# Two transposes of a gated attention layer by 32x32 blocks and DRAM, a permuted token order of the residual, and a build-time clock that orders the stages

## The chip, the cores and the metric

The kernel runs on one core of a Trainium2 chip. That core has a matrix engine (TensorE; PE in the profile, with its weight loads shown apart as PEld), a vector engine (VectorE, DVE), an activation engine (ScalarE, ACT), a general engine (GpSimd, POOL) and a queue that issues DMAs (SyncE, SP). Each engine works through its own instructions in the order in which the program lists them; semaphores tie the engines together. The metric is the device time of one execution in microseconds (us), as a median of several runs.

## The reference

A layer norm without weights feeds an attention layer and a feed-forward layer in parallel, and both results are added to the input. There are 8 sequences of 256 tokens, width 256, 16 heads of 128, and 64 slots (`M`) per head. Cut to what matters:

```python
xn = (x - mean) / sqrt(var + 1e-5)
# attention, per head
q, k = rope(xn @ Wq.T), rope(xn @ Wk.T);  v = xn @ Wv.T;  g = xn @ Wg.T
s   = clip(xn @ Ws1.T @ Ws2.T + bs2, -32, 32)         # [T, 64]
es, enz = exp(s), exp(-cumlogsumexp(s over tokens))
A   = tril(q @ k.T) * 128**-0.5
ok  = enz * (A @ es)                                   # logits over 64 slots
qv  = softmax(ok)
W2  = tril((qv * enz) @ es.T)
o   = W2 @ v
o   = o * rsqrt(mean(o*o) + 1e-5) * g_norm * silu(g)
attn = concat_heads(o) @ Wo.T
# feed-forward, weights stored as 4-bit codes with one scale per 32
ffn = (gelu(xn @ Wgate.T) * (xn @ Wup.T)) @ Wdown.T
out = x + attn + ffn
```

All of it is computed in float32.

## The kernel before, in words

The 2048 tokens are cut into 4 groups of 512 (`G`), and a group into 4 chunks of 128 (`TC`). The heads are taken in pairs, so there are 4 groups x 8 pairs = 32 attention steps `n`. The steps are pipelined by hand: while step `n` computes values, gates, scores, logits and softmax, step `n + 1` gets its states and its rotated q and k, step `n - 1` gets its weights, outputs and so on, and `close` projects the outputs of an even and an odd step together. The feed-forward layer (`ffn`, L344) is a generator of 160 items (a gate block, an up block or a pair of down chunks each) that are dealt out among the steps. The 4-bit weights are decoded once into SBUF, 24 parts in all, in between.

**What sets the order.** The kernel schedules by hand: each stage function emits its matmuls at once, and puts what follows on the other engines into a `chain`, a generator that stops at `yield`. After each stage `tick` (L98) advances every open chain by one piece, in the order in which they were opened. `need` (L93) ticks until given chains are finished; `new` (L104) does so for the users of a buffer that is taken again, and the eight PSUM banks are such buffers (`bank`, L123). Within a step the stages are sorted by a place between 0 and 1, from the tables `POS`, `START`, `FEED`, `NORM_AT`; `FIRST`, `LAST` and `DUE` say how many feed-forward items and decoded parts each step gets.

**The logits and the softmax.** `logits` (L542) leaves 64 slots of two heads on the 128 partitions and 512 tokens along the free axis, and `ok` is that times `enz` (L560). The softmax needs tokens on partitions: `softmax` (L565) turns `ok` with four TensorE transposes of 128x128 into a PSUM bank (L572), takes the maxima (L580), and runs eight exponentials with their sums (L584). `turn` (L594), in the next step, transposes the result back with four more (L601) and multiplies it by `enz` (L605). `weights` (L632) waits for it.

**The outputs.** `outputs` (L674) applies the weights, normalizes and gates into `og` (L704), which has tokens on partitions. `turn_blocks` (L364) transposes its 32x32 blocks in place on VectorE (L366), and `exchange` (L368) moves the blocks to their places by a trip through DRAM: four stores of 64 KB (L371), and one load of 256 KB into `ogT` (L376). In `og` and `ogT` the four chunks of a token's place lie innermost, so that one chunk of `ogT` is read at a stride of four elements, which `close` does when it loads it as the weights of its matmuls (L728).

**Other lines that are named below.** `rope` (L462) projects q and k; `vg` (L514) values and gates; `ffn_block` (L298, L318) and `ffn_down` (L338) the feed-forward; `scores` (L532, L535); `states` (L424); `norm` (L205) the transposes of the normalized input into `xT`; `add_to` (L277) adds a PSUM bank to the residual `res`, and `added` (L266) stores two chunks when their last sum is in (L270); `load_w` (L161) loads a step's weights into a single buffer.

Of the kernel before, what the change touches and what calls it, by code (L numbers as in the profile page):

```python
# [32 lines left out]
POS = {'scores': (0.059, 0.112),  # L33
 'turn': (0,),
 'logits': (0.178,),
 'softmax': (0.232,),
 'cross': (0.179,),
 'weights': (0.179, 0.193),
 'low': (0,),
 'states': (0.223,),  # L40
 'outputs': (0.364, 0.394),
 'close': (0.107, 0.365),
 'rope': (0.36, 0.45, 0.487, 0.63),
 'vg': (0.458, 0.566, 0.766, 0.838)}
START = {-1: {'states': (0.544,), 'rope': (0.14, 0.43, 0.53, 0.63)},
 0: {'vg': (0.0, 0.03, 0.06, 0.229),
     'scores': (0.2, 0.28),
     'states': (0.342,),
     'logits': (0.34,),
     'softmax': (0.5,),  # L50
     'rope': (0.198, 0.24, 0.32, 0.45)}}
FEED = {-1: (0.452, 1.0)}
NORMS = {0: 1, 2: 2, 5: 3}
NORM_AT = (0.29, 0.293, 0.427, 0.58, 0.75, 0.938)
FIRST = [0.35, 1.41]
LAST = [2.16, 2.05]
DUE = [4, 6, 7, 7, 8, 8, 9, 10, 11, 12, 12, 13, 14, 15, 15, 16, 17, 18, 19, 19, 19, 22, 23, 23, 24]
# [3 lines left out]
def layer_kernel(ctx: ExitStack, tc: tile.TileContext, a: dict, out: bass.AP):  # L61
# [27 lines left out]

    chains = []  # L90
    held = {}

    def need(*gens):  # L93

        while any(c in chains for c in gens):
            tick()

    def tick():  # L98

        for c in list(chains):  # L100
            if next(c, chains) is chains:
                chains.remove(c)

    def new(pool, shape, tag, bufs=1, dtype=F32):  # L104

        users = held.setdefault(tag, [])
        if len(users) >= bufs:
            need(*users[-bufs])
        t = pool.tile(shape, dtype, tag=tag, name=tag, bufs=bufs)
        users.append([])  # L110
        at_tag[id(t)] = t, users[-1]
        return t

    at_tag = {}

    def chain(gen, *tiles):

        chains.append(gen)
        for t in tiles:
            at_tag[id(t)][1].append(gen)  # L120
        return gen

    def bank():  # L123
        return new(ps_p, [P, 512], "ps", 8)
# [24 lines left out]

    def load_x(t, k):  # L150

        nc.sync.dma_start(
# [4 lines left out]
    def load_w(n, k):  # L157

        if n < N:
            w = aw.tile([P, 2, 2, 2 * DK], F32, tag=f"wts{k}", name=f"wts{k}")  # L160
            nc.sync.dma_start(out=w, in_=a["wqkvg"][steps[n][1]][:, k : k + 2])  # L161
            wts[n, k] = w

# [20 lines left out]
    def norm(g, h):  # L184
# [5 lines left out]
        for i in range(2):  # L190
            nc.vector.bn_stats(st[:, i, :], res[:, g * TC + h + i, :])
            nc.vector.bn_aggr(mv[:, i, :], st[:, i, :])
        nc.vector.tensor_scalar(rstd, mv[:, :, 1], EPS, None, ALU.add)
        nc.gpsimd.tensor_tensor(rstd, rstd, nhalf[:, 0:2], ALU.pow)
        yield
        for i in range(2):
            nc.vector.tensor_scalar(
                xn[:, i, :], res[:, g * TC + h + i, :], mv[:, i, 0:1],
                rstd[:, i : i + 1], ALU.subtract, ALU.mult,
            )  # L200
        yield
# [6 lines left out]
        t = g * G + h * P  # L208

        def work():  # L210
            nc.scalar.copy(xT[:, :, t : t + 2 * P], ps.rearrange("p (c t) -> p c t", c=2))  # L211
            yield

        normed.setdefault(g, []).append(chain(work(), ps, xn))
        yield
# [6 lines left out]
    def load_packed(m):  # L222

        if m < 12:
# [4 lines left out]
            packed[m] = pk, sc  # L229

    def decode_next():
# [16 lines left out]
        def work():  # L248
            for k, left in enumerate((28, 24)):
# [3 lines left out]
            yield  # L253
            nc.vector.tensor_scalar(u, u, 0x81C00000 - (1 << 32), None, ALU.bitwise_and)
            nc.vector.scalar_tensor_tensor(
                w, u.bitcast(F32), 2.0 ** 126, sc.unsqueeze(1).to_broadcast([P, 2, CH]),
                ALU.mult, ALU.mult,
            )

        parts.append(chain(work(), pks, scs, u))  # L260
# [5 lines left out]
    def added(t):  # L266

        done[t] = done.get(t, 0) + 1
        if done[t] == left:
            nc.sync.dma_start(  # L270
# [610 lines left out]
```

## Time and profile before

| what | us |
|---|---|
| median of 3 runs (1251.34 to 1254.29) | 1252.76 |
| the profiled execution | 1250.65 |
| its span in the trace | 1248.6 |
| DVE busy | 866.9 (69%) |
| ACT busy | 508.5 (41%) |
| POOL busy | 442.4 (35%) |
| TensorE clock granted | 0.999 of full speed |

The span is the time from the first to the last instruction of the trace; some 2 us of the profiled execution's own time lie around it. A float32 matmul shows as two instructions, so that counts of matmuls in the rows are twice those in the code (the transposes are not doubled). The duration of a matmul is the time from its start to a modelled end, and successive matmuls overlap; what a matmul costs the engine is therefore read from start to start.

### The profile page before, as it was taken

What the parts mean: (1) busy time and instruction counts of PE and PEld (TensorE: products, weight loads), DVE (VectorE), ACT (ScalarE), POOL (GpSimd) and SP (SyncE); (2) the same over time, 40 slices, a digit from 0 to 9 for tenths busy, and PEclk for the clock granted to TensorE, in tenths of its full rate; (3) what the DMA queues carried; (4) which work ended last, traced back from release to release, by engine and by line L of the source; (5) the groups of instructions that cost most, each with busy time, mean ns of one, the idle gap of its engine ahead of it and who ended that gap; (6) DMA issues with size and microseconds to landing.
All of it is one profiled execution on the core that took longest, in us unless ns stands there. A gap on an engine that the chain in (4) does not pass through costs nothing.

```text
span 1248.6 us, 18213 instructions
## 1 busy us (share of the span) xinstructions
PE 1222.9 (98%) x6448; PEld 889.8 (71%) x6448; DVE 866.9 (69%) x1656; ACT 508.5 (41%) x1645; POOL 442.4 (35%) x408
## 2 busy tenths in 40 slices
PE   6999899999999999999999999999999999999997
PEld 3566677777777777767777686776777777777775
DVE  4987667786676778675787757766766677676553
ACT  3354334444344444343443534345443244444321
POOL 3525344333244432334442333444232344332311
PEclk9999999999999999999999999999999999999999
DMA  5104222112222212122221122222112222211211
GB/s 159 64 11 142 85 69 85 26 50 78 85 69 68 84 27 59 53 68 85 78 60 35 54 64 85 68 68 53 33 51 69 68 68 68 63 41 51 67 51 51
DMA packets 64514, 81.55 MB, mean 65 GB/s; under 512 B 7140, under 2 KB 44388, under 8 KB 64424
## 3 DMA queue, kind: packets, MB, share of 16 engines
q1 hardware_dynamic: 63992, 80.13, 22.5%
q8 instruction: 51, 0.84, 0.3%
q14 instruction: 39, 0.32, 0.1%
q10 hardware_dynamic: 432, 0.26, 0.1%
HBM read 61.49 MB, written 18.87 MB: 64 GB/s over the span
## 4 chain that ended last, share of the span: by engine, by line
PE 92%; DVE 4%; DMA 2%; issue 1%; ACT 1%; POOL 0%; ACTq 0%; SPq 0%; DVEq 0%; POOLq 0%
PE ps L514 17%; PE ps L462 17%; PE ps L728 10%; PE ps L338 9%; PE ps L318 8%; PE ps L298 8%; PE ps L683 4%; PE ps L532 4%; PE ps L551 4%; PE ps L642 3%; PE ps L535 2%; PE ps L424 2%; PE ps L572 1%; PE ps L619 1%; DMA pk<-in_codes_dram 1%; PE ps L668 1%
## 5 line engine op out<-in xcount | busy, mean ns | idle before, releaser
L475 POOL TENSOR_TENSOR z<-z,sin 128x512 f32<-128x512 f32 x128 | 164.3, 1284 | 380.7 <-ACT z L472 380.2
L462 PE MATMUL ps<-xT,wts 128*128 128x512 f32 x512 | 242.7, 597 | 0.7 <-ACT xT L211 0.7
L514 PEld LDWEIGHTS ps<-wts,xT 128*128 128x128 f32 x1024 | 194.3, 190 | 65.1 <-issue 37.5
L514 PE MATMUL ps<-wts,xT 128*128 128x256 f32 x1024 | 236.5, 379 | 0.0
L462 PEld LDWEIGHTS ps<-xT,wts 128*128 128x128 f32 x512 | 94.0, 191 | 79.3 <-issue 71.3
L471 ACT COPY z<-ps 64x512 f32<-64x512 f32 x128 | 74.5, 582 | 138.4 <-PE ps L462 80.3
L728 PE MATMUL ps<-w_o,ogT 128*128 128x256 f32 x512 | 127.0, 402 | 0.0
L728 PEld LDWEIGHTS ps<-w_o,ogT 128*128 128x128 f32 x512 | 122.5, 328 | 2.3 <-issue 1.2
L298 PE MATMUL ps<-xT,w_gate 128*128 128x512 f32 x256 | 120.7, 594 | 2.7 <-DVE q L473 2.7
L318 PE MATMUL ps<-xT,w_up 128*128 128x512 f32 x256 | 120.6, 593 | 0.4 <-DVE k L473 0.4
L338 PE MATMUL ps<-w_down,inter 128*128 128x256 f32 x512 | 116.4, 380 | 4.4 <-DVE inter L326 4.4
L451 DVE RECIPROCAL enz<-enz 128x128 f32<-128x128 f32 x128 | 116.7, 932 | 0.0
L306 POOL TENSOR_SCALAR t<-t 128x512 f32<-128x512 f32 x64 | 40.4, 631 | 213.9 <-ACT t L304 206.4
L338 PEld LDWEIGHTS ps<-w_down,inter 128*128 128x128 f32 x512 | 96.1, 190 | 18.9 <-DVE inter L326 5.6
L277 DVE TENSOR_TENSOR res<-ps,res 128x512 f32<-128x512 f32 x64 | 43.2, 679 | 82.4 <-PE ps L338 46.8
L476 POOL TENSOR_TENSOR k<-k,z 128x512 f32<-128x512 f32 x64 | 81.5, 1273 | 48.2 <-DVE k L473 44.8
L700 POOL TENSOR_TENSOR ss<-ss,nhalf 128x4 f32<-128x4 f32 x64 | 64.8, 1014 | 94.0 <-DVE ss L699 92.0
L704 DVE SCALAR_TENSOR_TENSOR og<-ps,ss,sgate 128x128 f32<-128x128 f32 x256 | 78.4, 434 | 19.8 <-POOL ss L700 19.8
L310 ACT ACTIVATE t<-t 128x512 f32<-128x512 f32 x64 | 40.3, 630 | 123.7 <-DVE t L308 123.7
L476 POOL TENSOR_TENSOR q<-q,z 128x512 f32<-128x512 f32 x64 | 81.5, 1273 | 21.7 <-DVE q L473 15.8
L308 DVE TENSOR_TENSOR t<-ps,t 128x512 f32<-128x512 f32 x64 | 43.3, 677 | 55.3 <-POOL t L306 55.3
L584 ACT ACTIVATE pr<-ps,mx 128x64 f32<-128x64 f32 x256 | 76.2, 323 | 12.8 <-DVE mx L581 10.4
(79 smaller groups left out, 1931.8 us busy)
## 6 DMA issues: line engine op xcount, KB each, us to landing
wts<-in_wqkvg_dram SPq DMA_DIRECT2D x64, 512.0 KB, 4.5
by_way<-og SPq DMA_DIRECT2D x256, 64.0 KB, 1.8
ogT<-by_way SPq DMA_DIRECT2D x64, 256.0 KB, 2.7
pk<-in_codes_dram SPq DMA_DIRECT2D x12, 256.0 KB, 10.3
sc<-in_scales_dram SPq DMA_DIRECT2D x12, 256.0 KB, 10.3
w_o<-in_wo_dram SPq DMA_DIRECT2D x4, 512.0 KB, 5.5
out_dram<-res SPq DMA_DIRECT2D x8, 256.0 KB, 2.2
res<-in_x_dram SPq DMA_DIRECT2D x3, 512.0 KB, 10.2
```

The source lines that it names most:

```text
L298: nc.tensor.matmul(pg, lhsT=w_gate[:, c, ns], rhs=xT[:, c, gs], start=c == 0, stop=c == 1)
L318: nc.tensor.matmul(pu, lhsT=w_up[:, c, ns], rhs=xT[:, c, gs], start=c == 0, stop=c == 1)
L338: nc.tensor.matmul(ps[:, k, :], lhsT=inter[g, n][0][:, (i + k) * P : (i + k + 1) * P], rhs=w_dn[:, n, :], start=n == 2 * q, stop=n == 2 * ...
L451: nc.vector.reciprocal(r, r)
L462: nc.tensor.matmul(ps, lhsT=w[:, c, :], rhs=xT[:, c, g * G : (g + 1) * G], start=c == 0, stop=c == 1)
L471: nc.scalar.copy(z[0:64], pv[64:128])
L475: nc.gpsimd.tensor_tensor(z, z, sin_b, ALU.mult)
L476: nc.gpsimd.tensor_tensor(y, y, z, ALU.add)
L514: nc.tensor.matmul(ps[:, k, :], lhsT=xT[:, c, tt], rhs=w[:, which, c, :], start=c == 0, stop=c == 1,)
L584: nc.scalar.activation(pr[:, k, :], pv[:, k, :], AF.Exp, bias=mx[:, k : k + 1], scale=SCALE, accum_out=sm[:, k : k + 1],)
L704: nc.vector.scalar_tensor_tensor(og[:, :, i], po[:, i, :], ss[:, i : i + 1], sg[:, i, j * DK : (j + 1) * DK], ALU.mult, ALU.mult,)
L728: nc.tensor.matmul(ps[:, k, :], lhsT=ogT[hh][0][:, :, i + k], rhs=w_o[:, (hp // 2) * 4 + hh, :], start=hh == 0, stop=hh == 3,)
```

## The change

The change has four parts.

**1. The logits and the softmax are turned by blocks and DRAM.** The eight TensorE transposes of a step, the stage `turn` and the two PSUM banks go. A helper `turned` does what `turn_blocks` and `exchange` did (one 32x32 block transpose on VectorE, four stores, one load), and is used for `ok`, for the exponentials `pr` and for `og`. The maxima are taken in two instructions from SBUF and the exponentials read SBUF. The multiplication by `enz` after the way back moves from VectorE to GpSimd. The four tiles involved have one buffer each, and two of them are taken again within the chain (`again`).

**2. The blocks are contiguous.** `og`, `ogT`, `ok` and `pr` are laid out as (block, chunk, 32), so that the transpose reads and writes runs, and `close` reads each chunk of `ogT` contiguously. The tokens of a chunk come out in another order, so the residual `res` and `x` use that order (the host permutes `x`); `inter` is written permuted, `xT` is written back in the natural order in two copies of ScalarE instead of one, and the final store of two chunks is eight stores of 32 rows instead of one.

**3. A clock at build.** A chain now yields the engine and an assumed cost before each piece, each stage adds an assumed TensorE cost, and pieces are emitted in the order of their assumed start times, up to the assumed TensorE time; `need` moves that time forward. Ranks (0 to 2) break ties. The clock exists at build only; the chip sees another order of the same kinds of instructions. The tables of places, `FIRST`, `LAST`, `NORM_AT` and `DUE` have other values.

**4.** A factor of 0.5 moves from the product of the feed-forward into the decoded down weights.

```diff
-POS = {'scores': (0.059, 0.112),
- 'turn': (0,),
- 'logits': (0.178,),
- 'softmax': (0.232,),
- 'cross': (0.179,),
- 'weights': (0.179, 0.193),
+POS = {'scores': (0.057, 0.067),
+ 'logits': (0.14,),
+ 'softmax': (0.303,),
+ 'cross': (0.15,),
+ 'weights': (0.182, 0.257),
...
+    def V(n):
+        return "v", 0.15 + 0.00105 * n
+    def S(n):
+        return "s", 0.15 + 0.00088 * n
+    def pe(t):
+        clock["pe"] += t
+    def begin(c):
+        if isinstance(c.what, Chain):
+            return float("inf") if c.what in chains else max(c.at, c.what.at)
+        return max(clock[c.what[0]], c.at)
+    def advance(until=None):
+        while chains:
+            c = min(chains, key=lambda c: (begin(c), c.rank))
+            t = begin(c)
+            if until is not None and t > until:
+                return
+            if isinstance(c.what, Chain):
+                c.at = t
+            else:
+                e, cost, *lag = c.what
+                clock[e] = t + cost
+                c.at = t + cost + (lag[0] if lag else 0.1)
+            c.what = next(c.gen, None)
+            if c.what is None:
                 chains.remove(c)
+            if until is None:
+                return
+    def need(*cs):
+        while any(c in chains for c in cs):
+            advance()
+        clock["pe"] = max([clock["pe"]] + [c.at for c in cs])
...
-            nc.scalar.copy(xT[:, :, t : t + 2 * P], ps.rearrange("p (c t) -> p c t", c=2))
+            for c in range(2):
+                nc.scalar.copy(xv[:, c, :, h : h + 2], pv[:, c])
...
         if done[t] == left:
-            nc.sync.dma_start(
-                out=out[t * P : (t + 2) * P, :].rearrange("(i p) d -> p i d", p=P),
-                in_=res[:, t : t + 2, :],
-            )
+            yield "d", 0.9
+            for k in (t, t + 1):
+                rows = out[k // TC * G : (k // TC + 1) * G].rearrange("(i r k) d -> r i k d", i=4, r=4)
+                for i in range(4):
+                    nc.sync.dma_start(
+                        out=rows[k % TC, i], in_=res[32 * i : 32 * (i + 1), k, :]
+                    )
...
-            nc.vector.scalar_tensor_tensor(it, t, 0.5, pu, ALU.mult, ALU.mult)
+            nc.vector.tensor_tensor(
+                it.rearrange("p (r i k) -> p i r k", r=4, i=4),
+                t.rearrange("p (i r k) -> p i r k", r=4, i=4),
+                pu.rearrange("p (i r k) -> p i r k", r=4, i=4), ALU.mult,
+            )
...
-    def turn_blocks(t):
-        v = t.rearrange("p (c k) i -> p c i k", c=4)
-        nc.vector.transpose(v, v)
-    def exchange(to, t):
+    def turned(to, t):
+        yield "v", 0.8
+        flat = t.rearrange("p c i k -> p (c i k)")
+        nc.vector.transpose(flat, flat)
+        yield "d", 1.75, 2.6
         by_way = dram.tile([P, 4, 32 * TC], F32, tag="by_way", name="by_way", bufs=4)
         for r in range(4):
             nc.sync.dma_start(
                 out=by_way.rearrange("(c k) r x -> r k c x", c=4)[r],
-                in_=t[32 * r : 32 * (r + 1)].rearrange("p (c k) i -> p c (k i)", c=4),
+                in_=t[32 * r : 32 * (r + 1)].rearrange("p c i k -> p c (i k)"),
             )
-        yield
+        yield "d", 0.4, 4.2
         nc.sync.dma_start(
-            out=to.rearrange("p t i -> p (t i)"), in_=by_way.rearrange("p r x -> p (r x)")
+            out=to.rearrange("p r i k -> p (r i k)"), in_=by_way.rearrange("p r x -> p (r x)")
         )
...
+        pe(0.86)
         of[n][tag, j] = y, chain(work(), ps, y, z)
...
-        ok = to["ok"] = new(p1, [P, G], "ok")
-        def work():
-            nc.vector.tensor_tensor(ok, ps, enz, ALU.mult)
-            yield
-        to["logits"] = chain(work(), ps, ok, enz)
+        ok = new(p1, [P, 4, TC, 32], "ok")
+        okT = to["okT"] = new(p1, [P, 4, TC, 32], "okT")
+        def work():
+            yield V(512)
+            nc.vector.tensor_tensor(
+                ok.rearrange("p c i k -> p i c k"), ps.rearrange("p (i c k) -> p i c k", i=TC, c=4),
+                enz.rearrange("p (i c k) -> p i c k", i=TC, c=4), ALU.mult,
+            )
+            yield from turned(okT, ok)
+        pe(1.4)
+        to["logits"] = chain(work(), ps, ok, okT, enz, rank=0)
     def softmax(n):
-        need(to["logits"])
-        ps = bank()
-        for i in range(TC):
-            ts = slice(i * P, (i + 1) * P)
-            nc.tensor.transpose(ps[:, ts], to["ok"][:, ts], ident)
...
+            yield to["logits"]
+            for j in range(2):
+                yield V(256)
+                nc.vector.tensor_reduce(
+                    mx[:, j * TC : (j + 1) * TC],
+                    okT[:, 2 * j : 2 * j + 2].rearrange("p c i k -> p i c k"), AX.XY, ALU.max,
+                )
+            yield "v", 0.17
             nc.vector.tensor_scalar(mx, mx, -SCALE, None, ALU.mult)
+            pr = again(p1, [P, 4, TC, 32], "ok", to["softmax"])
+            for j in range(2):
+                yield "s", 2.16
+                for i in range(TC):
+                    k, js = j * TC + i, slice(2 * j, 2 * j + 2)
+                    nc.scalar.activation(
+                        pr[:, js, i, :], okT[:, js, i, :], AF.Exp, bias=mx[:, k : k + 1],
+                        scale=SCALE, accum_out=sm[:, k : k + 1],
+                    )
...
-    def turn(n):
-        need(to["softmax"])
-        for i in range(TC):
-            nc.tensor.transpose(ps[:, i * P : (i + 1) * P], prf[:, i * P : (i + 1) * P], ident)
-            nc.vector.tensor_tensor(prT, ps, enz, ALU.mult)
+            prX = again(p1, [P, 4, TC, 32], "okT", to["softmax"])
+            yield from turned(prX, pr)
+            yield "g", 1.27
+            prT = to["prT"] = again(p1, [P, G], "prT", to["softmax"])
+            nc.gpsimd.tensor_tensor(
+                prT.rearrange("p (i c k) -> p i c k", i=TC, c=4),
+                prX.rearrange("p c i k -> p i c k"),
+                enz.rearrange("p (i c k) -> p i c k", i=TC, c=4), ALU.mult,
+            )
...
     def weights(n):
-        need(to["turn"])
+        need(to["softmax"])
...
-                    ps[:, k, :], lhsT=ogT[hh][0][:, :, i + k],
+                    ps[:, k, :], lhsT=ogT[hh][0][:, i + k],
...
-            tick()
+            advance(clock["pe"])
```

## The prediction

> **What bounds the kernel.** I read the first two blocks of the page, then busy time by stretch, then TensorE's timeline.
>
> ```profile
> PE 1222.9 (98%) x6448; PEld 889.8 (71%) x6448; DVE 866.9 (69%) x1656; ACT 508.5 (41%) x1645; POOL 442.4 (35%) x408
> ...
> PE   6999899999999999999999999999999999999997
> ```
>
> TensorE looks full from the third slice to the last but one. The stretches (busy us of each engine) say how full:
>
> ```profile
> 0.00:35.00 35.00, 24.40 (x79) 13.43 (x80) 18.42 (x36) 9.52 (x15) 13.52 (x22) 1.00 0.48 147
> 35.00:70.00 35.00, 30.71 (x132) 17.99 (x130) 33.39 (x68) 15.26 (x39) 15.35 (x14) 1.00 0.16 54
> 70.00:140.00 70.00, 66.36 (x358) 46.39 (x359) 52.79 (x107) 31.37 (x103) 32.01 (x29) 0.98 0.34 106
> 140.00:600.00 460.00, 460.00 (x2503) 340.27 (x2501) 327.44 (x626) 191.68 (x630) 161.64 (x145) 1.00 0.22 61
> 600.00:1100.00 500.00, 500.00 (x2662) 368.24 (x2662) 348.52 (x663) 211.31 (x691) 185.43 (x165) 1.00 0.22 63
> ```
>
> From 140 us on TensorE has no idle time, and its list of waits between 140 and 1226 us is empty. So in 32 pipelined steps (22 of them, from the `close` at 363.32 to that at 1169.36 in the chain of waits, take 806.04 us, or 36.64 each) a microsecond of TensorE work is a microsecond of the span, and work elsewhere is free until it makes TensorE wait. Idle are 18.5 us before 140 us (35 - 24.40, 35 - 30.71, 70 - 66.36; 7.4 are the wait for the first input) and 3.3 us near the end (L338, below).
>
> Busy time overstates what a matmul costs, since successive ones overlap. The timeline of TensorE (start, length, group) gives the cost from start to start:
>
> ```profile
> 616.70 3.62 PE L514 MATMUL ps<-wts,xT 128*128 128x256 f32 x16
> 620.15 1.88 PE L298 MATMUL ps<-xT,w_gate 128*128 128x512 f32 x4
> 621.87 0.60 PE L601 MATMUL ps<-ident,pr 128*128 128x128 f32 x4
> 622.31 0.60 PE L532 MATMUL ps<-q,k 128*128 128x256 f32 x2
> ...
> 630.82 0.66 PE L572 MATMUL ps<-ident,ok 128*128 128x128 f32 x4
> 631.32 1.88 PE L462 MATMUL ps<-xT,wts 128*128 128x512 f32 x4
> ```
>
> **Removed: the eight transposes.** L601 takes 0.44 us (621.87 to 622.31), L572 0.50 (630.82 to 631.32). 0.94 x 32 steps = **30.1 us**, all on the path. The 1.9 us for which L601 waits (before 140 us) go with it; behind them stand L532's own inputs, so I count them gone, with 0 as the other bound.
>
> **Contiguous weights of `close`.** These rows differ only in the stride of the operand:
>
> ```profile
> L728 PEld LDWEIGHTS ps<-w_o,ogT 128*128 128x128 f32 x512 | 122.5, 328 | 2.3 <-issue 1.2 <-DVE inter L326 0.2
> L338 PEld LDWEIGHTS ps<-w_down,inter 128*128 128x128 f32 x512 | 96.1, 190 | 18.9 <-DVE inter L326 5.6 <-issue 1.0
> ```
>
> In the chain of waits 16 matmuls of L728 take 3.84 us and 16 of L338 3.46. With the load at 190 ns the first should cost what the second does: 0.38 x 32 groups = **12.2 us**. Here a rule speaks against the change: the Trainium skill ("TensorE: Matmul & The Clock Gate", "LDWEIGHTS (loading the stationary operand)") lets the time of a load depend on the number of columns alone, which is 128 in both rows; by it the stride costs nothing and the gain is 0. The trace has 328 against 190 ns; I take the row, and 0 goes into the range.
>
> A second rule is against the first part: "VectorE: DVE Perf Modes", "Rules for kernel authors", sends a 128x128 transpose to TensorE where PSUM may be the target, and keeps VectorE for blocks of 32x32. By it the 30.1 us stay and the detour only adds latency: the sum would be 1240. But TensorE is the engine with no idle time, and VectorE has 29% (327.44 of 460 us busy), so here the slower way is the cheaper one.
>
> **Added on VectorE.** Per step two block transposes. Nearest row: L366 at 1152 ns, read and written at a stride of four; contiguous ones should take between 0.69 (the 512-element L326 row) and 1.15. With the two of `og`, 128 at 0.69 to 1.15 minus 73.7 now: +15 to +74 us; two smaller maxima instead of one at most +22 (680 ns again); less 21.9 for L605. That makes 860 to 941 us of some 1210, at most 78%: not a bound. GpSimd gets 32 x 1.27 (the L476 row) = 41 us, to 40%. ScalarE's exponentials stay; eight extra halves of the `xT` copy are at most 5 us on 41%. The other reshaped products keep their element counts, and the factor 0.5 removes no instruction: nothing, covered by idle time on VectorE.
>
> **Added on the DMA queue.** Two trips per step: 256 stores and 64 loads more. A trip moves 0.5 MB, so 33.5 MB on top of 81.55; the queue's share of the engines rises from 22.5% to about 32%. SP issues per step 8 x 0.43 + 2 x 0.34 = 4.1 us more. These share SP with the weight loads (L161), which wait there for TensorE to let the buffer go (50.0 + 25.4 us in all, longest 13.2), and whatever is queued behind waits too.
>
> **The new wait, and its cover.** `weights` waited for the transposes; now it waits for a chain of nine pieces. From the trace: logits' matmuls 1.35 (626.74 to 628.09), product 0.69, trip 7.2 (the `og` transpose at 608.21 to its load issued at 612.68, plus 2.7 to landing), maxima 0.9 to 1.4, scaling 0.17, eight exponentials with their reads 8 x 0.54 = 4.3, `eps` 0.15, second trip 7.2, product on GpSimd 1.27: 23 to 24 us. Its cover is what TensorE does between `logits` at place 0.14 and `weights` at 0.182 of the next step: a whole step, 36.64 - (30.1 + 12.2) / 32 = 35.3 us, plus `cross` 0.54 and `states` 0.66 between them, 36.5. About 12 us are left for queueing on VectorE, ScalarE, GpSimd and SP. Without cover every microsecond costs 32. Single buffers of `ok` and `okT` ask for less: they are free again once the second trip has been read.
>
> **The order.** All else in the steady part can move only within the idle time of the other engines; TensorE cannot gain there (it waits for nothing) but can lose. One thing speaks against the new order: the clock prices `rope` at 0.86 where the timeline has 1.72 from start to start (L298, the same shape: 620.15 to 621.87), `close` at 1.73 against 3.84, `scores` at 0.65 against 1.3; shared-array stages such as `logits` (1.4 against 1.35) are right. The order is made for a TensorE about twice as fast, and so for a VectorE that lags behind it. Real slack is then larger than assumed, which favours no waits; but a piece that was put behind another one, because both were thought late, can keep a bank busy. I take 0; bounds: gain 11 (the 11.1 us idle before 140 us beyond the first input) plus 3.3 at the end, loss about 0.5 us per step, 16 (waits of TensorE on VectorE before 140 us are 0.3 to 2.3 us each).
>
> ```profile
> PE ps L205 <- DVE z L197: 10.3, 3, 7.4
> PE ps L338 <- DVE inter L326: 4.4, 3, 2.1
> PE ps L298 <- DVE q L473: 2.7, 2, 2.1
> ```
>
> These three are most of what TensorE waits for (us in all, times, longest); none lies between 140 and 1226 us.
>
> **The end.** The last sum ends at 1245.45, and one store (issue 0.43, 2.2 to landing) closes the span at 1248.6. Now eight follow each other: seven more issues at 0.43 (median of the L371 issues) = **+3.0**; bounds 2.1 (0.30 each) and 8.2 (1.17, the longest). The eight of the other half begin some 3.7 us earlier and are just out. Earlier groups' stores hide.
>
> **Sum**, against the profiled execution: 1250.65 - 30.1 - 12.2 - 1.9 + 3.0 = 1209.5. The median of the runs lies 2.1 higher, so I name **1210**.
>
> **Rivals.**
> A. As forecast, and the start gets better too, since loads of `x` and of the codes now have landing times in the clock and the first steps' places are new. For: 11.1 us idle there, 3.3 at the end. Against: the first codes land late whatever the order (10.3 us from issue), and every other piece competes with the start-up. Two thirds of the 14.4: 1200.
> B. TensorE waits in the steady part for pieces ordered by the wrong prices, 0.5 us a step: 1210 + 16 = 1226. For: the halved prices. Against: VectorE's 29% idle time.
> C. The stride doesn't matter (the rule above): 1210 + 12.2 = 1222.
> D, slower: the chain from `logits` to `weights` doesn't fit a step. Place: L642 waiting for the product on GpSimd. Price: 24 us plus queueing, 31 times over what passes 36.5. The gain of some 41 us is spent at 41 / 31 = 1.3 us, so from a chain of 37.8 us on it is slower. It takes, for instance, 6.2 us (the longest wait of a weight load for L514) ahead of each trip's stores and 3 us more at the hand-overs: 39.4, or 2.9 x 31 = 90, which makes 1300. For: single buffers, an in-order SP that now does four trips a step. Against: 12 us of slack.
> E. The blocks don't replace the transposes but leave the count of matmuls as it was: excluded by the code, which emits none in `softmax`.
>
> **Chances.** Forecast 0.55, A 0.17, B 0.13, C 0.07, D 0.08. The range **1197 to 1230** takes in A, B and C with the tail's bounds and leaves D out. A measurement of this kernel can tell 0.2% from no change (2.5 us, about the spread of the three runs). Only D is slower, 0.07 with 0.01 for a D that just balances: faster 0.92, same 0.01, slower 0.07.
>
> **What would show it.** TensorE instructions 256 fewer (6448 to 6192), as 128 + 128 transposes go. L728's successor: loads at 190 ns, 16 matmuls in 3.46 us. Busy 100% from about 140 us, no waits of the `weights` matmuls on GpSimd. Steps of 35.3 us. VectorE near 900 us, block transposes 0.7 to 1.15 us each. DMA bytes near 115 MB. Last store landing 5 to 6 us after the last sum. The prediction is wrong if `weights`, or banks behind VectorE, show waits in each step, or if the loads of `close` stay at 328 ns.

## The result, and the profile after

The changed kernel takes 1242.76 us (median of 4 runs, 1241.07 to 1243.06), the kernel before 1252.17 in the same comparison: ratio 0.992, 95% interval 0.9902 to 0.9937. It is faster, by 9.4 us where about 42 were forecast, and lies 12.8 us above the end of the range. The profiled execution took 1241.07 us, with a span of 1239.3.

The first two blocks of the page of the changed kernel, with its DMA queue and the two rows of `close` (L841, L728 before):

```profile
PE 1202.6 (97%) x6192; PEld 838.2 (68%) x6192; DVE 891.9 (72%) x1720; ACT 516.0 (42%) x1653; POOL 484.7 (39%) x440
...
PE   6899899999999999999999999899999999999996
...
PEclk9989999999999999999999999899999999999998
...
q1 hardware_dynamic: 110968, 113.71, 34.2%
...
L841 PE MATMUL ps<-w_o,ogT 128*128 128x256 f32 x512 | 115.7, 379 | 0.0
...
L841 PEld LDWEIGHTS ps<-w_o,ogT 128*128 128x128 f32 x512 | 96.5, 190 | 20.5 <-issue 8.1
```

The 256 instructions are gone (6448 to 6192), and the loads of `close` fell from 328 to 190 ns, so the work removed is the work forecast. But TensorE has a slice at 8 in the middle, and its granted clock dips in the same slice and near the start. Busy time by stretch of the changed kernel (columns as before: PE, PEld, DVE, ACT, POOL, then granted clock, DMA share, GB/s):

```profile
0.00:35.00 35.00, 25.25 (x80) 14.12 (x81) 18.32 (x37) 10.35 (x18) 13.86 (x23) 0.95 0.44 139
35.00:70.00 35.00, 28.94 (x112) 16.08 (x111) 34.59 (x67) 15.35 (x40) 15.11 (x14) 0.90 0.26 80
70.00:140.00 70.00, 64.24 (x345) 43.55 (x344) 56.05 (x115) 31.36 (x103) 36.49 (x33) 1.00 0.48 129
140.00:600.00 460.00, 459.33 (x2436) 324.59 (x2437) 346.42 (x661) 197.35 (x637) 182.70 (x160) 1.00 0.34 92
600.00:1100.00 500.00, 496.03 (x2607) 346.95 (x2606) 363.02 (x698) 217.72 (x698) 199.90 (x177) 0.99 0.35 92
```

From 140 to 1100 us TensorE now idles 4.6 us (0.67 + 3.97) where it idled 0, and the start got no better: from 35 to 70 us VectorE is busy 34.59 of 35 us, so there it is the bound, and TensorE does less in that time (28.94 us at a clock of 0.90, against 30.71 at 1.00). Its waits (us in all, times, longest):

```profile
PE ps L279 <- DVE z L261: 16.8, 3, 7.1
PE ps L423 <- DVE inter L407: 7.4, 5, 2.6
PE ps L515 <- DMA w_s<-in_ws_dram: 2.2, 1, 2.2
PE ps L423 <- DVE at L623: 1.9, 1, 1.9
```

None of them is the new chain. `weights` (L748) waits for nothing; GpSimd's product stands in front of its trip for 22.7 us in all, and TensorE does not feel it.

**Where the time went.** The start of each `close` in TensorE's timeline cuts the span into four: up to the first `close`, 28 steps, the last `close` but one to the last, the tail. These are profiled executions (that of the contiguous blocks alone was its slowest, 3.3 us above its median); the two kernels in the last rows come back in the experiments.

| | first close at | 28 steps (one) | to the last close | tail | span |
|---|---|---|---|---|---|
| before | 140.1 | 1029.1 (36.75) | 67.9 | 11.5 | 1248.6 |
| changed kernel | 155.1 | 1012.7 (36.17) | 57.7 | 13.8 | 1239.3 |
| contiguous blocks alone | 138.9 | 1020.1 (36.43) | 67.9 | 13.8 | 1240.7 |
| changed kernel, TensorE transposes back | 157.4 | 1038.0 (37.07) | 56.5 | 14.3 | 1266.2 |

Forecast was a step of 35.43 in these terms (36.75 less 0.94 and 0.38). Measured is 36.17: 0.74 x 28 = 20.7 us are missing there. The start took 15.0 us longer and the stretch to the last `close` 10.2 us less; together that is 4.8 longer where four steps' share of the gains should have made it about 5 shorter. Most of the two numbers is a shift of the cut itself: the new tables put the first `close` of a step at 0.348 of it instead of 0.107. Cut at `weights`, whose place hardly moved (0.179 to 0.182), the third of them starts at 149.0 us before and at 149.6 after, 28 steps take 1029.0 and 1014.5, and what follows takes 70.6 and 75.1 us. So the start brought nothing, and the end lost 4.5 us, the longer tail included.

### The profile page after: what moved, and what is told of

Its sections match the earlier page's. It is cut to its first block, busy times and chain, and to the rows that moved or that the text cites. A ratio compares the mean times of both kernels' runs of the same rounds, so it can differ in the third digit from the quotient of the medians.

```text
span 1239.3 us, 18558 instructions
## 1 busy us (share of the span) xinstructions
PE 1202.6 (97%) x6192; PEld 838.2 (68%) x6192; DVE 891.9 (72%) x1720; ACT 516.0 (42%) x1653; POOL 484.7 (39%) x440
## 4 chain that ended last, share of the span: by engine, by line
PE 86%; DVE 9%; DMA 2%; issue 1%; POOL 1%; ACT 0%; POOLq 0%; DVEq 0%; SPq 0%; ACTq 0%
PE ps L556 16%; PE ps L613 15%; PE ps L423 9%; PE ps L841 9%; PE ps L376 8%; PE ps L398 7%; PE ps L632 4%; PE ps L791 4%; PE ps L652 4%; PE ps L748 3%; PE ps L635 2%; PE ps L515 2%; PE ps L775 1%; DVE enz L543 1%; DMA pk<-in_codes_dram 1%
## 5 line engine op out<-in xcount | busy, mean ns | idle before, releaser
L556 PE MATMUL ps<-xT,wts 128*128 128x512 f32 x512 | 248.7, 609 | 0.5 <-ACT xT L289 0.5
L556 PEld LDWEIGHTS ps<-xT,wts 128*128 128x128 f32 x512 | 92.1, 192 | 79.6 <-issue 69.8
L423 PE MATMUL ps<-w_down,inter 128*128 128x256 f32 x512 | 122.0, 392 | 9.4 <-DVE inter L407 7.4
L695 ACT ACTIVATE ok<-okT,mx 128x64 f32<-128x64 f32 x256 | 85.6, 337 | 91.2 <-DVE mx L689 86.6
L398 PE MATMUL ps<-xT,w_up 128*128 128x512 f32 x256 | 123.1, 604 | 0.0
L572 POOL TENSOR_TENSOR q<-q,z 128x512 f32<-128x512 f32 x64 | 81.5, 1273 | 94.8 <-DVE q L569 69.7
L423 PEld LDWEIGHTS ps<-w_down,inter 128*128 128x128 f32 x512 | 98.9, 196 | 26.4 <-DVE inter L407 9.7
L841 PE MATMUL ps<-w_o,ogT 128*128 128x256 f32 x512 | 115.7, 379 | 0.0
L349 DVE TENSOR_TENSOR res<-ps,res 128x512 f32<-128x512 f32 x64 | 44.0, 688 | 93.9 <-PE ps L423 57.7
L841 PEld LDWEIGHTS ps<-w_o,ogT 128*128 128x128 f32 x512 | 96.5, 190 | 20.5 <-issue 8.1
L543 DVE RECIPROCAL enz<-enz 128x128 f32<-128x128 f32 x128 | 108.5, 909 | 0.0
L817 DVE SCALAR_TENSOR_TENSOR og<-ps,ss,sgate 128x128 f32<-128x128 f32 x256 | 75.3, 344 | 45.9 <-POOL ss L813 45.9
L566 ACT COPY z<-ps 64x512 f32<-64x512 f32 x128 | 74.5, 582 | 73.0 <-PE ps L556 63.8
L572 POOL TENSOR_TENSOR k<-k,z 128x512 f32<-128x512 f32 x64 | 82.6, 1290 | 20.6 <-DVE k L569 16.9
L623 DVE TENSOR_TENSOR at<-ps,mask 128x384 f32<-128x384 f32 x128 | 65.4, 552 | 26.4 <-PE ps L635 26.0
```

Source lines behind the costliest of these rows:

```text
L398: nc.tensor.matmul(pu, lhsT=w_up[:, c, ns], rhs=xT[:, c, gs], start=c == 0, stop=c == 1)
L423: nc.tensor.matmul(ps[:, k, :], lhsT=inter[g, n][0][:, (i + k) * P : (i + k + 1) * P], rhs=w_dn[:, n, :], start=n == 2 * q, stop=n == 2 * ...
L543: nc.vector.reciprocal(r, r)
L556: nc.tensor.matmul(ps, lhsT=w[:, c, :], rhs=xT[:, c, g * G : (g + 1) * G], start=c == 0, stop=c == 1)
L566: nc.scalar.copy(z[0:64], pv[64:128])
L572: nc.gpsimd.tensor_tensor(y, y, z, ALU.add)
```

## The experiments

The question is which part ate the gain: the trips, the clock at build, its prices, or the tables of places. A kernel is either in **the order of before** (one piece per chain after each stage), or **under the clock**, with the old or the new tables. Ratios are against the kernel before, with 95% intervals.

### Contiguous blocks alone

The kernel before with parts 2 and 4 of the change:

```diff
-        ogT = new(p2, [P, P, TC], "ogT", 4)
+        ogT = new(p2, [P, 4, TC, 32], "ogT", 4)
...
-                    ps[:, k, :], lhsT=ogT[hh][0][:, :, i + k],
+                    ps[:, k, :], lhsT=ogT[hh][0][:, i + k],
```

> The kernel before with the contiguous blocks alone (layout of og and ogT, token order of the residual, eight stores at the end); TensorE transposes and the old order stay. If the stride is a TensorE cost as the loads' rows say: 12.2 us less and 3 us more at the end, 1243 against 1252, and 16 matmuls of close in 3.46 us. If the stride costs nothing: 1252 to 1256.

1239.47 us, ratio 0.9898 (0.9881 to 0.9914). These two parts gain 12.7 us alone (against the 1252.17 of the result), more than the whole change does. In its timeline of TensorE 16 matmuls of `close` (L738 here) take 3.45 us from start to start, as forecast from L338:

```profile
650.49 3.62 PE L738 MATMUL ps<-w_o,ogT 128*128 128x256 f32 x16
653.94 0.59 PE L540 MATMUL ps<-q,k 128*128 128x256 f32 x2
```

So the rule weighed in the prediction (the Trainium skill, "TensorE: Matmul & The Clock Gate", "LDWEIGHTS (loading the stationary operand)"), that the columns alone set a load's time, does not hold for this stride, and rival C falls. Parts 1 and 3 on top of it made the kernel 3 us slower, though part 1 removes 30 us of TensorE's work.

### The changed kernel without the clock, and with true prices

First the tables of the change with the order of before's rule (one piece per chain after each stage), then the change with the clock told what TensorE really takes.

```diff
-            c = min(chains, key=lambda c: (begin(c), c.rank))
-            t = begin(c)
-            if until is not None and t > until:
-                return
+        for c in list(chains):
```

> The changed kernel with the old rule of order (after each stage every open chain advances by one piece) in place of the clock; all operations and the tables of places stay. Theory 1 (the order made by the clock loses what the transposes gave): 1210 to 1225, clearly under the changed kernel's 1242.8. Rival (the loss is in the operations themselves, as VectorE's longer work and the split TensorE sequence, whatever the order): 1235 to 1250. Rival 2 (the clock is what keeps TensorE fed): over 1250.

1312.22 us, ratio 1.0477 (1.0459 to 1.0494). With the new tables the clock is worth 69 us: these tables need it.

```diff
-        pe(0.86)
+        pe(1.72)
...
-        pe(1.73)
+        pe(3.46)
```

> The changed kernel with the clock's TensorE prices set to what the trace shows (1.72 for 0.86, 3.46 for 1.73, 1.3 for 0.65, 0.9 for 0.46). If pieces stand behind others because the clock takes TensorE for twice as fast: 1220 to 1232, and the waits near 58, 133 and 794 us shrink. If the order of pieces isn't what makes TensorE wait: 1240 to 1246.

1241.49 us, ratio 0.9907 (0.9892 to 0.9922), against 0.992 (0.9902 to 0.9937) for the change. The halved prices, on which I rested rival B, are not the cause. With true ones the waits near 794 us shrink to one of 0.9 us, but the two long waits of the start stay and shorter ones come elsewhere ("PE ps L652 <- DVE at L623: 4.7, 8, 1.3").

### The clock with TensorE's transposes

The change with its trips taken out again: eight TensorE transposes per step, the stage `turn`, two banks; then the same with the old tables.

```diff
-            yield from turned(okT, ok)
...
+            nc.tensor.transpose(ps[:, ts], to["ok"][:, ts], ident)
...
+            nc.tensor.transpose(ps[:, i * P : (i + 1) * P], prf[:, i * P : (i + 1) * P], ident)
```

> The changed kernel with the eight TensorE transposes of a step back, everything else (clock, tables, contiguous blocks) as changed. Theory 1 (the clock and its tables lose 28 us whatever they order): 1265 to 1272, slower than before. Theory 2 (the clock's order is as good as the old one, the loss comes with the trips): 1238 to 1244, as the contiguous blocks alone.

1268.19 us, ratio 1.013 (1.0113 to 1.0147).

> The sixth experiment's kernel (clock, contiguous blocks, TensorE transposes) with the tables of before, so that TensorE's own order is the old one and the clock orders the other engines alone; the norms keep two pieces, at 0.29 and 0.58 and their turns at 0.75 and 0.938. If the new tables (TensorE's order) cost the 28.7 us between the first and the sixth experiment: 1238 to 1246. If the clock's order of the other engines costs them: 1260 to 1275.

1255.94 us, ratio 1.0031 (1.0018 to 1.0044), between the two forecasts. Both do the same work as the contiguous blocks alone (1239.47), in another order. So with transposes the order costs 28.7 us: 16.5 by the clock with the old tables, 12.3 more by the new ones. And under the new order the trips are worth 1268.2 - 1242.8 = 25.4 us; a step falls from 37.07 to 36.17, by 0.90, against 0.94 forecast. The gain is there in the step; the order had taken it beforehand.

### The trips in the order of before

If the order costs that much, the trips should go into the old one. Chains of before stop only at `yield`; so each wait for a trip was put some idle ticks (n) behind the load.

The core of it, on top of the contiguous blocks alone, with the transposes and `turn` taken out:

```diff
+            turn_blocks(pr)
+            yield
+            yield from exchange(prX, pr)
+            for _ in range(n):
+                yield
+            nc.gpsimd.tensor_tensor(
...
```

Three idle ticks before the maxima and before the product, then none:

> The first experiment's kernel (contiguous blocks, old order and tables) with the eight TensorE transposes of a step replaced by the two trips through DRAM, three idle ticks before each use of what a trip brings. Theory 1 (the trips are worth 28 us, the loss is in the new order and tables): 1210 to 1222. Theory 2 (the trips themselves cost about what they save, since the longer chain and VectorE's extra pieces make TensorE wait and cool): 1232 to 1250.

> The fifth experiment's kernel without the idle ticks, so that VectorE's and GpSimd's uses stand where the trip has often not landed. If VectorE held up by a trip is what stalls TensorE: 10 us or more over the fifth. If there is slack for it: within 4 us of it.

1283.65 us, ratio 1.0259 (1.0239 to 1.0279), with three, slower than either forecast; 1396.57 us, ratio 1.117 (1.1132 to 1.1208), with none. The trips now cost 44 and 157 us. Waits of the kernel with three, of TensorE and of GpSimd:

```profile
PE ps L546 <- POOL k L490: 30.1, 13, 4.3
...
POOL prT L623 <- DMA okT<-by_way: 130.5, 29, 9.8
```

GpSimd's timeline in one step of it (start, length, group, idle time before it):

```profile
327.48 1.27 POOL L623 TENSOR_TENSOR prT<-okT,enz 128x512 f32<-128x512 f32 x1 [7.13 <-DMA okT<-by_way]
328.71 1.26 POOL L489 TENSOR_TENSOR z<-z,sin 128x512 f32<-128x512 f32 x1
330.05 1.27 POOL L490 TENSOR_TENSOR k<-k,z 128x512 f32<-128x512 f32 x1
331.27 1.26 POOL L489 TENSOR_TENSOR z<-z,sin 128x512 f32<-128x512 f32 x1
332.61 1.27 POOL L490 TENSOR_TENSOR q<-q,z 128x512 f32<-128x512 f32 x1
333.84 1.27 POOL L489 TENSOR_TENSOR z<-z,sin 128x512 f32<-128x512 f32 x1
335.19 1.26 POOL L490 TENSOR_TENSOR k<-k,z 128x512 f32<-128x512 f32 x1
```

The product stands 7.13 us in its wait; the six pieces of the rotation behind it start late, and TensorE's scores wait for the last of them. Without idle ticks VectorE stands in the same way ("DVE mx L599 <- DMA okT<-by_way: 113.6, 31, 5.5"). At this point two readings were left: the place of that wait, or something else that trips do to the old order.

### The same, with the product later

Only the number of idle ticks before the product changes, from three to eight and to fourteen; then eight with the product on VectorE.

```diff
-            for _ in range(3):
+            for _ in range(8):
                 yield
             nc.gpsimd.tensor_tensor(
```

> The order of before with contiguous blocks and both trips, as in the run at 1283.65 us, but the product on GpSimd is put eight ticks behind its trip instead of three. If what that order loses is GpSimd standing in the wait for the trip ahead of the pieces of the rotation (130.5 us of waiting there, TensorE's scores then 30.1 us late and its clock falling after each wait), the later place takes most of the 130.5 us away and the time falls towards that of contiguous blocks alone less the transposes: 1215 to 1245. If the trips cost the old order through something else (VectorE's larger load, the DMA queue), it stays within 10 us of 1283.

> As the run before, fourteen ticks behind. By the first theory no worse than with eight unless the weights stage is reached first, when the remaining ticks are run off in a row and the wait comes back: 1215 to 1260. By the second, near 1283.

> Eight ticks behind, but the product on VectorE (32 x 0.7 us more there, 41 us less on GpSimd). If only the place in the queue counts, the same as with eight ticks on GpSimd within 8 us. If GpSimd itself is short of time for the rotation, faster than that by over 8 us; if the wait now stands on VectorE ahead of the PSUM readers, slower.

| ticks before the product | us | ratio (95%) |
|---|---|---|
| 3, GpSimd | 1283.65 | 1.0259 (1.0239 to 1.0279) |
| 8, GpSimd | 1231.97 | 0.9828 (0.9809 to 0.9847) |
| 14, GpSimd | 1232.68 | 0.9838 (0.9824 to 0.9853) |
| 8, VectorE | 1231.23 | 0.9829 (0.9815 to 0.9844) |

One instruction put later takes 51.7 us away. GpSimd in the same step, with eight ticks:

```profile
320.93 1.28 POOL L490 TENSOR_TENSOR k<-k,z 128x512 f32<-128x512 f32 x1 [0.68 <-DVE k L487]
322.16 1.27 POOL L489 TENSOR_TENSOR z<-z,sin 128x512 f32<-128x512 f32 x1
323.51 1.26 POOL L490 TENSOR_TENSOR q<-q,z 128x512 f32<-128x512 f32 x1
325.80 1.26 POOL L623 TENSOR_TENSOR prT<-okT,enz 128x512 f32<-128x512 f32 x1 [1.02 <-DMA okT<-by_way]
327.02 1.26 POOL L489 TENSOR_TENSOR z<-z,sin 128x512 f32<-128x512 f32 x1
```

Pieces of the rotation now go ahead of it, and it waits 1.02 us. Its waits for the trip fall from 130.5 to 21.2 us in all, and L490 no longer stands in TensorE's list of waits. GpSimd is not short of time, since the product on VectorE gives the same. So the old order carries the trips, and the new one is not needed for them: with trips in both, the changed order stands at 1242.8 and the old one at 1232.0.

### Where the new order loses: places and waits

The same stretch of a step, TensorE's timeline of the changed kernel:

```profile
623.29 1.16 PE L748 MATMUL ps<-prT,esT 64*128 64x128 f32 x16
624.38 1.98 PE L556 MATMUL ps<-xT,wts 128*128 128x512 f32 x4
626.29 0.71 PE L775 MATMUL ps<-cross,prT 64*128 64x128 f32 x8
626.94 1.98 PE L556 MATMUL ps<-xT,wts 128*128 128x512 f32 x4
628.76 1.05 PE L791 MATMUL ps<-v,wt 128*128 128x128 f32 x8
```

and of the contiguous blocks alone (L650 and L676 are the same two stages):

```profile
623.60 1.16 PE L650 MATMUL ps<-prT,esT 64*128 64x128 f32 x16
624.60 0.61 PE L676 MATMUL ps<-cross,prT 64*128 64x128 f32 x8
625.14 0.38 PE L432 MATMUL ps<-w_s,rT 17*128 17x128 f32 x2
```

In the old order the stages that use 64 or 17 rows of the array stand together. The new one puts a stage of 128 rows (here `rope`) between them, and at every passage between the two kinds the start-to-start time is longer: L748 1.09 against 1.00 us, the first L556 1.91 against 1.72 (its usual distance), L775 0.65 against 0.54, the second L556 1.82. That is 0.09 + 0.19 + 0.11 + 0.10 = 0.49 us a step less 0.05 for a passage that the old order has too (L580 behind L432), some 12 us over 28 steps. The same distances stand in nearly every step. No wait shows it, and TensorE counts as busy. To test it, `apply` (L775) was put back beside `weights`; in a second run `states` was put behind both.

```diff
- 'weights': (0.182, 0.257),
+ 'weights': (0.182, 0.182),
```

The second run:

```diff
- 'weights': (0.182, 0.257),
+ 'weights': (0.182, 0.183),
...
- 'states': (0.167,),
+ 'states': (0.19,),
```

> The changed kernel with the second part of the weights stage (apply) at the place of the first (0.182 for 0.257), so that the matmuls of 64 rows stand together again. If each passage between matmuls of 64 and of 128 rows costs TensorE 0.1 to 0.2 us, as the start-to-start times suggest (0.3 us a step): 1232 to 1236. If not: 1240 to 1246.

> The changed kernel with weights at 0.182, apply at 0.183 and states at 0.19, so that cross, weights, apply and states stand side by side as before. If the passages between matmuls of part of the array and of all of it cost the 0.3 us a step that the start-to-start times show: 1233 to 1238. If not: 1240 to 1246.

1242.1 us, ratio 0.9912 (0.9897 to 0.9927): no gain. The two passages go, but `apply` now waits in the middle of its matmuls (0.34 us in one step) for VectorE to copy `states` out ("DVE esT L526") and takes 0.90 us from start to start on average instead of 0.65; and from 140 to 1100 us TensorE idles 13.0 us instead of 4.6. With `states` behind both 1324.07 us, ratio 1.0569 (1.0551 to 1.0588): there VectorE stands 119.6 us in the wait for `okT` (L684), and TensorE's scores wait 39.3 us for L572. Moving stages also moves the other engines' queues, so the passages could not be changed alone, and their 12 us stay a reading of the timeline, which no run confirms. What speaks for it: waits hardly tell the two kernels with trips apart. Behind the first input TensorE waits 22.6 us in the changed one and 22.7 in the old order with the product eight ticks late, at 10.5 and 8.1 us of lost clock (worked out at the end), yet 28 steps take 1012.7 and 1004.0 us.

The other place is a burst of waits near 790 us. The timeline of TensorE, VectorE and GpSimd of the changed kernel, cut:

```profile
789.55 2.19 DVE L328 TENSOR_SCALAR u<-pk 128x256 int32<-128x256 int32 x2
790.27 1.33 POOL L706 TENSOR_TENSOR prT<-okT,enz 128x512 f32<-128x512 f32 x1
...
793.82 1.94 DVE L623 TENSOR_TENSOR at<-ps,mask 128x384 f32<-128x384 f32 x4
794.42 1.83 PE L423 MATMUL ps<-w_down,inter 128*128 128x256 f32 x6 [1.93 <-DVE at L623]
798.20 4.21 PE L423 MATMUL ps<-w_down,inter 128*128 128x256 f32 x9 [1.95 <-DVE inter L407]
```

A part of the weights is decoded ahead of what TensorE waits for; the two steps there take 78.3 us from `close` to `close`, their neighbours 71.5 to 71.9. Two runs moved what the start and this burst wait for: decoding given rank 1 instead of 2, and the second norm at 0.56 instead of 0.78.

> The changed kernel with the decoding of weights at rank 1 instead of 2, so that decoded parts no longer come last among equals and pile up in front of a need. If VectorE's slow decoding (shifts of 841 ns, 298 before, while GpSimd works) in a bad place makes the burst of waits near 794 us and those of the start: 1230 to 1238. If not: 1240 to 1246.

> The changed kernel with the second half of each later norm placed at 0.56 of its step instead of 0.78 (its transposes stay at 0.92). If TensorE's two longest waits (5.15 us at 58, 4.58 us at 133, both for the normalized input) and the half clock behind them are the start's loss: 1231 to 1236, at least one of the two gone. If VectorE, which is full between 35 and 70 us, delays the norm wherever it is placed: 1240 to 1246 with the waits still there.

1240.07 us, ratio 0.9903 (0.9888 to 0.9918), and 1242.57 us, 0.9918 (0.9904 to 0.9933): neither differs from the change beyond the intervals. But the waits largely stayed: those for the normalized input behind the first sum to 9.1 and 6.2 us (9.7 in the change), the second run has a new one of 4.0 us for a decoded part ("PE ps L423 <- DVE w_down L334: 4.0, 1, 4.0"), and the one of 1.9 us near 794 us stands in both. So what these waits cost is not tested by them.

### The trips under the clock with the old tables

> The changed kernel (clock, trips) with the tables of before. If the tables cost TensorE what the sixth experiment lost, and the chain fits a step under the clock: 1212 to 1225. If the new places are what makes the trips fit: 1245 or more.

1314.29 us, ratio 1.0504 (1.0474 to 1.0533), with "DVE mx L684 <- DMA okT<-by_way: 146.9, 30, 6.7": here the maxima come too soon. The runs together, in us:

| order | TensorE transposes | trips |
|---|---|---|
| of before | 1239.5 | 1283.7; product later 1232.0 |
| clock, old tables | 1255.9 | 1314.3 |
| clock, new tables | 1268.2 | 1242.8 |

### Versions that beat both

Under the clock: the earlier norm, the decoding rank, four parts' due times evened out, and the eight stores at the end issued by SyncE's and ScalarE's queues in turn. In the old order: the product on VectorE eight ticks late, and the same split of the stores.

```diff
-                    nc.sync.dma_start(
+                    (nc.scalar if i % 2 else nc.sync).dma_start(
```

> The changed kernel with four edits: that norm place, decoding at rank 1, the due counts smoothed so that no step decodes three parts (19, 20, 21, 22 for 18, 19, 19, 22), and the final stores split over two issuing queues. If the waits found in the trace are the loss: 1224 to 1232, with the burst near 794 us gone and about 1.5 us off the end. If they only move elsewhere: 1236 to 1242.

> The run with the product on VectorE eight ticks late (1231.23 us), with the last eight stores of each pair of chunks issued by two queues in turn, SyncE's and ScalarE's. If the tail is the issuing of seven more stores one after the other (forecast 3.0 us), half of it goes: 1229 to 1230.5. If the stores end by their landing or ScalarE is held by the issuing elsewhere, no gain or up to 2 us slower.

1236.07 us, ratio 0.9868 (0.9853 to 0.9883), and **1229.70 us, ratio 0.9833 (0.982 to 0.9846)**. The second is the fastest measured, 22 us below the kernel before and 13 below the changed one. In the first the two steps of the burst take 74.5 us instead of 78.3. What the split of the stores gives shows in the traces: from the last sum's end to the span's end it is 4.0 us in both, 6.0 without the split. In the medians of the second (1231.23 to 1229.70) it lies within the intervals.

## Why the prediction was wrong

- **What bounds the kernel, and the two gains: right.** TensorE's work is the span. The contiguous blocks gave 12.7 us with the longer tail in it, where 12.2 less 3.0 was forecast, so 3.5 more; in the profiled executions a step falls by 0.32 (0.38), and where the rest of the 12.7 comes from is open. The transposes gave 0.90 us a step (0.94) under the new order. VectorE's block transposes take 0.70 us, its load is 72%, GpSimd's 39%, the queue moves 115 MB: all as forecast.
- **The tail: right.** From the last sum's end (1233.26) to the span's end 6.0 us, before 3.15: +2.9 against +3.0.
- **The chain and its cover (rival D): right for this order.** `weights` never waits; by the starts in the trace GpSimd's product comes 24.7 to 33.0 us after the logits began, the weights 31.6 to 44.4 us after. In the tightest step 3 us lie between the product's end and the weights, where 12 were forecast. But the argument was about length alone, 24 us in a cover of 36.5, and that is not what decides. The same chain, in about the same cover, costs 44 or 157 us in the old order if its waits stand at the wrong place of GpSimd's or VectorE's queue. I had named SP as the in-order queue to fear; it was the engines at the ends of the trips.
- **The order: this is the step that failed.** "I take 0; bounds: gain 11 ... loss about 0.5 us per step, 16." With the transposes in place the new order costs 28.7 us, outside the bound; with trips in both it costs 10.8 against the old order with the product later, inside it. The 0 stood for an order packed as tightly as before, and no order that was run, the old one included, is that with the trips in it. My argument was that work elsewhere may move freely while TensorE waits for nothing. It missed that the order also decides what stands next to what on TensorE itself (passages that count as busy; by the timeline about a third of the 28.7 us), that a start in which VectorE is full (33.39 of 35 us, a number that I showed) has no room to gain, and that short waits are not priced at their length (below). Rival B had the right sign and the wrong cause: true prices bring nothing. The 1240 that the rule for transposes would have given lies near the measured 1242.8 by luck: the trips do bring their gain, and the order takes it away.
- **The sum.** Of the forecast step of 35.43 us 0.74 are missing: about 0.44 by passages, 6.5 / 28 = 0.23 by the burst near 790 us and 0.06 by the loads of `close`, as read from the timeline. The other 10 us are in the start and the end. (The sum itself was rounded in the change's favour: 1209.5 and the 2.1 for the median make 1211.6, not 1210.)
- **Open.** In the old order with the product later a step takes 1004.0 / 28 = 35.86 us, not 35.43, and the first `close` comes at 146.2 us instead of 138.9: the trips bring 7.5 us there, not 30. The start's own places were not fitted to the trips, and in some steps the logits now wait for VectorE's masked scores ("PE ps L565 <- DVE at L536: 2.7, 5, 0.7"); the transposes no longer stand between the two. Fitting these places was not tried.

## What to carry to other kernels

A chain that leaves an engine and comes back is not priced by its length against its cover alone: ask at which place of an in-order queue its wait stands, and what stands behind it; putting one such instruction later was worth 52 us here. When a change also reorders, do not take 0 for the order, but measure the reordering alone: a small net result was here a gain of 25 us and a loss of 29. And a local change that needs no new order (here the stride of an operand) can be the larger part of what remains.

## What the runs showed of the hardware

**A wait can cost more than its length.** Behind many single waits of TensorE of some 2 to 5 us the granted clock is low for some microseconds. Near the end of the changed kernel (timeline of TensorE, the last waits):

```profile
1214.04 0.70 PE L423 MATMUL ps<-w_down,inter 128*128 128x256 f32 x2 [1.13 <-DVE inter L407]
1217.33 8.29 PE L423 MATMUL ps<-w_down,inter 128*128 128x256 f32 x26 [2.59 <-DVE inter L407]
```

The 26 matmuls take 8.1 us from their start to that of `close` at 1225.46; at the usual distance of 3.46 per 16 they would take 5.6. It does not follow every such wait. These are the stretches after the same last wait in the kernel before (2.08 us, until 1231.38), in the contiguous blocks alone (2.07 us, until 1219.49) and in the changed kernel (2.59 us, above); the clock is the third number from the end:

```profile
1230.00:1235.00 5.00, 3.62 (x17) 3.21 (x18) 1.92 (x3) 0.00 (x0) 0.00 (x0) 1.00 0.33 80
1220.00:1225.00 5.00, 5.00 (x18) 4.13 (x17) 0.69 (x1) 0.00 (x0) 0.00 (x0) 0.68 0.21 56
1220.00:1225.00 5.00, 5.00 (x19) 4.19 (x18) 0.69 (x1) 0.00 (x0) 0.00 (x0) 0.78 0.20 52
```

In the first the 26 matmuls take 5.7 us. In windows of 5 us, busy time times what is missing of the clock adds up to 10.5 us for the changed kernel (nearly all in five places, at about 20, 65, 140, 797 and 1217 us, each at a wait, at clocks of 0.54 to 0.78), 1.2 for the one before, 3.1 for contiguous blocks alone and 19.1 for the trips at the wrong place. From the kernel before to the changed one TensorE's waits behind the first input rose from 14.5 to 22.6 us, so 8.1 us of added waits came with 9.3 us of lost clock. The ratio is no constant: the old order with the product eight ticks late waits 22.7 us with the product on GpSimd and 22.5 with it on VectorE, and loses 8.1 and 4.2 us of clock.

**VectorE's shifts last longer when they start under a GpSimd product of two tensors of 128x512.** The shift of the decoding, out of SBUF and into it, in the kernel before and in the changed one:

```profile
L250 DVE TENSOR_SCALAR u<-pk 128x256 int32<-128x256 int32 x48 | 12.3, 298 | 11.6 <-DMA pk<-in_codes_dram 11.6
L328 DVE TENSOR_SCALAR u<-pk 128x256 int32<-128x256 int32 x48 | 38.4, 841 | 12.0 <-DMA pk<-in_codes_dram 12.0
```

In the trace of the changed kernel 30 of the 48 shifts start while such a product runs on GpSimd; each of them ends 148 to 154 ns after that product does, and they take 1179 ns on average. The other 18 take 222 to 294 ns. In the old order with trips, with as much work on GpSimd, 3 of the 48 do (with the product eight ticks late), and the mean is 300: what counts is where the two meet.

**A stride of four elements in a transpose by blocks** costs 1152 ns for 128x512 in float32, contiguous blocks 704, both read and written in SBUF (before, then after):

```profile
L366 DVE STREAM_TRANSPOSE og<-og 128x512 f32<-128x512 f32 x64 | 73.7, 1152 | 2.2
L453 DVE STREAM_TRANSPOSE ok<-ok 128x512 f32<-128x512 f32 x64 | 45.1, 704 | 0.4
```
